# A transformer block on one core: the joining factors' two differences from one GpSimd subtraction with a reversed operand

## The chip, the cores and the metric

The kernel runs on one core of a Trainium2 chip. The metric is the device time of one execution in microseconds (us). The engines are named as the profile names them: PE (TensorE matmuls; PEld is its weight load), DVE (VectorE), ACT (ScalarE), POOL (GpSimd) and SP (SyncE, which here only issues DMAs). "SPq" is SP's queue of DMA issues. L517 is line 517 of the kernel before.

## The reference

All of it is fp32. x is (2, 1024, 256), the context (2, 154, 192), 16 heads of 64:

```python
h = _layernorm(x, ln1_g, ln1_b)
x = _attention(h, h, sa_wq, sa_wk, sa_wv, sa_wo, sa_bo) + x
h = _layernorm(x, ln2_g, ln2_b)
x = _attention(h, cond_emb, ca_wq, ca_wk, ca_wv, ca_wo, ca_bo) + x
h = _layernorm(x, ln3_g, ln3_b)
p = h @ ff_w1 + ff_b1
a, gate = (p[..., :D_FF], p[..., D_FF:])
h = a * jax.nn.gelu(gate, approximate=False) @ ff_w2 + ff_b2
return h + x
```

The attention is softmax(q k^T / 8) v over each head, followed by the output projection. The change lies in the softmax of the first attention, the self-attention, alone.

## The kernel before, in words

The program runs three stages one after the other: the self-attention (about 20 to 725 us of the profile), the cross-attention and the gated feed-forward. Each engine's instructions are written out by hand in a fixed order (`tc.manual_schedule()`, L1004), so that an instruction that waits holds up all that stands behind it on its engine.

**Self-attention.** A unit is one batch and one pair of heads; there are 16 units. Each unit takes 8 steps (L1062: `for p in range(SA)`, 128 steps in all), and a step handles two groups of 64 queries. In `scores` (L481, matmuls at L488) a group's score tile has 128 partitions: four blocks of 32 partitions, made of two sets of 32 queries by the two halves of the 1024 keys. A partition thus holds one query against one half of the keys (512), for both heads of the pair. The two halves of one query lie on two different blocks of partitions.

One step, `self_first(p)` (L642), goes as follows:

1. PE writes the scores of two groups into two PSUM tiles, L488. There are only two buffers, so that PE can write the next step's scores only when ACT has read these.
2. DVE takes the negated maximum over each half of the keys, L650, twice.
3. ACT takes the exponents with that maximum as bias and sums each row as it goes, L499, four times 128x512.
4. Four DMAs on SP's queue carry the maxima and sums to the partitions of the other half of the keys, `exchange`, L509.

The two halves of a query were scaled by different maxima. One step later they are joined (`scale_groups`, L590, which calls `join`, L513). `st` is a tile of [own or other half][maximum or sum][group, head], so 2 x 2 x 4 numbers on each partition. The join is a chain of tiny instructions:

- L517 and L518 on POOL: `dd` = the other half's negated maximum less the own one (first half of `dd`), and the reverse (second half), 128x4 each;
- L519 on POOL: the minimum of `dd` and 0, 128x8;
- L521 on ACT: `ee` = exp(dd), 128x8, which stands in ACT's order behind the four exponents of the current step;
- L523 on POOL: `zz` = ee times the sums, 128x8; L525 on POOL: `den` = the sum of both halves of `zz`, 128x4;
- L596 on DVE: `rd` = 1/den; then four times L600 on POOL: the exponents times `rd` and `ee`, 128x512.

DVE's order within a step is: two maxima (L650), two 32x32 block transposes of the weights scaled a step earlier (L614), sometimes the adding of an output projection (L469) or layer-norm statistics, and last the reciprocal L596. The maxima of the next step stand behind that reciprocal. PE's order within a step is: the scores, and then a piece of other work (the projections L357 and L388, the weighted values L535, the output projection L462).

What follows from the order is a loop over two steps: maxima, exponents, exchange by DMA, join, reciprocal, and behind the reciprocal the next maxima.

Of the kernel before, what the change touches and what calls it, by code (L numbers as in the profile page):

```python
# [10 lines left out]
ALU = mybir.AluOpType  # L11
# [7 lines left out]
def tile_transformer_block(ctx: ExitStack, tc: tile.TileContext, a: dict, out: bass.AP):  # L19
    nc = tc.nc  # L20
# [492 lines left out]
    def join(u, st):  # L513

        dd = small.tile([P, 2, 4], F32, tag="dd", name=f"dd_{u}")
        neg = st[:, :, 0].rearrange("p s i j -> p s (i j)")
        nc.gpsimd.tensor_tensor(dd[:, 0, :], neg[:, 1, :], neg[:, 0, :], ALU.subtract)  # L517
        nc.gpsimd.tensor_tensor(dd[:, 1, :], neg[:, 0, :], neg[:, 1, :], ALU.subtract)  # L518
        nc.gpsimd.tensor_scalar(dd, dd, 0.0, 1.0, op0=ALU.min, op1=ALU.mult)  # L519
        ee = small.tile([P, 2, 4], F32, tag="ee", name=f"ee_{u}")  # L520
        nc.scalar.activation(ee, dd, AF.Exp)  # L521
        zz = small.tile([P, 2, 4], F32, tag="zz", name=f"zz_{u}")
        nc.gpsimd.tensor_tensor(zz, ee, st[:, :, 1].rearrange("p s i j -> p s (i j)"), ALU.mult)  # L523
        den = small.tile([P, 4], F32, tag="den", name=f"den_{u}")
        nc.gpsimd.tensor_tensor(den, zz[:, 0, :], zz[:, 1, :], ALU.add)  # L525
        return ee, den
# [63 lines left out]
    def scale_groups(u, st, members):  # L590

        ee, den = join(u, st)

        def reciprocals():
            rd = small.tile([P, 4], F32, tag="rd", name=f"rd_{u}")
            nc.vector.reciprocal(rd, den)  # L596
            for i, pr in enumerate(members):
                for j in range(2):
                    c = 2 * i + j
                    nc.gpsimd.tensor_scalar(  # L600
                        pr[:, j, :], pr[:, j, :], rd[:, c:c + 1], ee[:, 0, c:c + 1],
                        op0=ALU.mult, op1=ALU.mult,
                    )
                groups.append(pr)

        return reciprocals
# [636 lines left out]
```

## Time and profile before

| what | value |
|---|---|
| time, median of 3 runs | 1113.07 us (1111.95 to 1114.58) |
| the profiled execution's own time | 1114.26 us |
| its span | 1112.5 us |
| self-attention, 20 to 720 us: busy PE / DVE / ACT / POOL | 690.3 / 634.2 / 463.3 / 526.8 of 700 us |
| instructions at L517, L518 | 128 each, 201 and 202 ns |
| granted TensorE clock, mean | 0.998 |

A busy time is the sum of an engine's instructions. A wait is the idle time of an engine before an instruction, put down to the one that released it. The chain of waits is followed back from the last instruction of the program: at each step to what released it, or to the instruction before it on its engine; what lies on it set the end of this execution, as far as the profile tells.

### The profile page before, as it was taken

How to read it: one execution, taken by the hardware profiler on the slowest of the kernel's cores; microseconds unless marked ns; L12 is line 12 of the kernel's file. 1: busy time of each engine (PE TensorE's matmuls, PEld its weight loads, DVE VectorE, ACT ScalarE, POOL GpSimd, SP SyncE). 2: the span in 40 equal slices, each digit the busy share in tenths (PEclk: the TensorE clock that was granted, in tenths of full speed). 3: DMA queues.
4: the chain of work that ended last, by engine and by line, in shares of the span. 5: the costliest groups of instructions: out<-in, count | busy, mean ns of one | idle time of the engine just before them, and what ended most of it. 6: DMA issues, size and time to landing. Idle time of an engine off the chain costs nothing.

```text
span 1112.5 us, 44903 instructions
## 1 busy us (share of the span) xinstructions
PE 1092.5 (98%) x18452; PEld 732.9 (66%) x18452; DVE 855.3 (77%) x1205; ACT 626.1 (56%) x2025; POOL 684.7 (62%) x1584
## 2 busy tenths in 40 slices
PE   8999999999999999999999999999999999999998
PEld 6555666556757555566565565566766677888887
DVE  4889999898988989999999989978777885422212
ACT  4666666766666656666666766565556553121111
POOL 2777777777878777777777877776656653220000
PEclk9999999999999999999999999999999999999999
DMA  2222212121112011111111111046765553000000
GB/s 81 69 56 58 56 28 52 41 53 42 34 42 49 14 41 37 33 42 33 32 42 24 41 33 26 21 98 159 166 153 136 117 116 79 10 11 10 20 10 19
DMA packets 103983, 60.73 MB, mean 55 GB/s; under 512 B 32218, under 2 KB 94562, under 8 KB 103778
## 3 DMA queue, kind: packets, MB, share of 16 engines
q1 hardware_dynamic: 102546, 57.20, 21.8%
q8 instruction: 146, 2.39, 0.9%
q10 hardware_dynamic: 1232, 0.66, 0.2%
q14 instruction: 59, 0.48, 0.1%
HBM read 27.91 MB, written 2.10 MB: 27 GB/s over the span
## 4 chain that ended last, share of the span: by engine, by line
PE 63%; ACT 9%; DMA 7%; POOL 7%; DVE 7%; issue 3%; SPq 3%; DVEq 0%; POOLq 0%; ACTq 0%
PE pa L959 10%; PE po L535 10%; PE s L488 10%; ACT p L499 8%; DMA st<-st 6%; PE pf L982 5%; PE py_ca L462 5%; DVE st L650 4%; PE pq_ca L357 4%; PE poc L877 4%; SPq L509 3%; PE py_sa L462 3%; PE sc L798 3%; PE pv_sa L388 3%; PE pk_sa L357 3%
## 5 line engine op out<-in xcount | busy, mean ns | idle before, releaser
L499 ACT ACTIVATE p<-s,st 128x512 f32<-128x512 f32 x512 | 345.3, 687 | 195.4 <-DVE st L650 185.2
L600 POOL TENSOR_SCALAR p<-p,rd,ee 128x512 f32<-128x512 f32 x512 | 387.7, 772 | 46.8 <-DVE rd L596 45.9
L650 DVE TENSOR_REDUCE st<-s 128x2 f32<-128x1024 f32 x256 | 300.9, 1216 | 22.6 <-PE s L488 9.7
L614 DVE STREAM_TRANSPOSE pT<-p 128x1024 f32<-128x1024 f32 x256 | 302.3, 1218 | 0.3 <-POOL p L600 0.3
L488 PE MATMUL s<-k_sa,q_sa 64*32 64x512 f32 x4096 | 263.9, 593 | 8.6 <-ACT p L499 7.6
L535 PE MATMUL po<-pT,v_sa 64*32 64x256 f32 x8192 | 241.2, 376 | 1.7 <-DVE pT L614 1.4
L535 PEld LDWEIGHTS po<-pT,v_sa 64*32 64x32 f32 x8192 | 178.1, 106 | 71.9 <-issue 19.2
L488 PEld LDWEIGHTS s<-k_sa,q_sa 64*32 64x32 f32 x4096 | 82.6, 106 | 113.5 <-ACT p L499 61.9
L814 ACT ACTIVATE p<-sc,neg 128x154 f32<-128x154 f32 x256 | 96.4, 406 | 83.5 <-DVE rden L822 78.4
L825 POOL TENSOR_SCALAR p<-p,rden 128x154 f32<-128x154 f32 x256 | 97.3, 401 | 71.6 <-DVE rden L822 71.3
L968 DVE SCALAR_TENSOR_TENSOR u<-pa,cols,gate 128x256 f32<-128x256 f32 x64 | 30.9, 483 | 123.1 <-ACT gate L965 123.1
L959 PE MATMUL pa<-hT_ln,wf 128*128 128x256 f32 x512 | 121.1, 380 | 0.0
L965 ACT ACTIVATE gate<-pa,cols 128x256 f32<-128x256 f32 x64 | 30.4, 475 | 147.4 <-PE pa L959 144.1
L959 PEld LDWEIGHTS pa<-hT_ln,wf 128*128 128x128 f32 x512 | 96.7, 190 | 13.8 <-issue 0.9
L499 ACT ACTIVATION_READ_ACCUMULATOR p<-s,st 128x1 f32 x512 | 103.9, 203 | 0.0
L388 PEld LDWEIGHTS pv_sa<-sa_wv,hT_ln 64*128 64x128 f32 x1024 | 59.0, 188 | 14.6 <-issue 5.0
L982 PE MATMUL pf<-wf,u 128*128 128x256 f32 x256 | 64.7, 379 | 0.0
L523 POOL TENSOR_TENSOR zz<-ee,st 128x8 f32<-128x8 f32 x128 | 26.0, 203 | 60.4 <-ACT ee L521 60.4
L388 PE MATMUL pv_sa<-sa_wv,hT_ln 64*128 64x128 f32 x1024 | 62.2, 275 | 0.3 <-ACT v_sa L397 0.3
L462 PE MATMUL py_sa<-sa_wo,o_sa 128*128 128x256 f32 x256 | 59.7, 385 | 0.0
L462 PE MATMUL py_ca<-ca_wo,o_ca 128*128 128x256 f32 x256 | 59.7, 381 | 0.0
L357 PE MATMUL pk_sa<-hT_ln,sa_wk 64*32 64x512 f32 x960 | 58.2, 591 | 1.0 <-DMA st<-st 0.8
(89 smaller groups left out, 1253.6 us busy)
## 6 DMA issues: line engine op xcount, KB each, us to landing
wf<-pT_ca SPq DMA_DIRECT2D x128, 128.0 KB, 2.4
st<-st SPq DMA_DIRECT2D x512, 1.0 KB, 1.8
v_sa<-v_sa SPq DMA_DIRECT2D x32, 256.0 KB, 3.8
sa_wq<-in_L_xattn_sa_wq_dram SPq DMA_DIRECT2D x32, 128.0 KB, 3.0
sa_wk<-in_L_xattn_sa_wk_dram SPq DMA_DIRECT2D x32, 128.0 KB, 2.9
sa_wv<-in_L_xattn_sa_wv_dram SPq DMA_DIRECT2D x32, 128.0 KB, 3.3
ca_wq<-in_L_xattn_ca_wq_dram SPq DMA_DIRECT2D x32, 128.0 KB, 3.8
wf<-in_L_xattn_ff_w_dram SPq DMA_DIRECT2D x12, 256.0 KB
```

Of the source, the lines that this page charges most:

```text
L357: nc.tensor.matmul(pq[r][f:f + m, at:at + n], lhsT=wt[own, c, f:f + m], rhs=h[own, c, t0:t0 + n], start=(c == 0), stop=(c == NH - 1), tile ...
L388: nc.tensor.matmul(pv[r][:, i * P:(i + 1) * P], lhsT=h[own, c, i * P:(i + 1) * P], rhs=wt[own, c, :], start=(c == 0), stop=(c == NH - 1), ...
L462: nc.tensor.matmul(py[:, e * D:(e + 1) * D], lhsT=o[:, i, (t + e) * P:(t + e + 1) * P], rhs=wo[kind][:, g * HP + i, :], start=(i == 0), st ...
L488: nc.tensor.matmul(sc[a4 * KB:(a4 + 1) * KB, j, :], lhsT=q[r, c:c + KB], rhs=k[r, h * HB:(h + 1) * HB], start=True, stop=True, tile_positi ...
L499: nc.scalar.activation(pr[:, j, :], sc[:, j, :], AF.Exp, bias=st[:, 0, 0, i, j:j + 1], accum_out=st[:, 0, 1, i, j:j + 1],)
L535: nc.tensor.matmul(po[a2][d:d + KB, :QH // 2], lhsT=v[r, t, e, d:d + KB], rhs=pT[r, d // DH * NK + n, :], start=(t == 0 and e == 0), stop= ...
L600: nc.gpsimd.tensor_scalar(pr[:, j, :], pr[:, j, :], rd[:, c:c + 1], ee[:, 0, c:c + 1], op0=ALU.mult, op1=ALU.mult,)
L614: nc.vector.transpose(halves[h][:, :, c:c + KB], groups.pop(0).rearrange("p j (n k) -> p (j n) k", k=KB))
L650: nc.vector.tensor_reduce(st[:, 0, 0, i, :], sc[i], AX.X, ALU.max, negate=True)
L825: nc.gpsimd.tensor_scalar(pr_[:, j, i, :T], pr_[:, j, i, :T], rden[:, j, i:i + 1], 1.0, op0=ALU.mult, op1=ALU.mult,)
L959: nc.tensor.matmul(pa[:, half, :TF * P], lhsT=w1[:, c, half * DF + f * P:half * DF + (f + 1) * P], rhs=h[:, c, t0 * P:(t0 + TF) * P], star ...
L982: nc.tensor.matmul(sums[blk][i][:, :D], lhsT=sums[blk, "u"][:, f, i * P:(i + 1) * P], rhs=w2[:, f, :], start=(f == 0), stop=(f == NF - 1),)
```

## The change

The two subtractions that write the two halves of `dd` become one that writes all of it. Its second operand is both halves in their order, its first the two halves in reverse order: on each partition 2 x 4 elements with steps of -8 and 1, from element 8 on, beside 2 x 4 elements with steps of 8 and 1 from element 0 on. The values are the same.

```diff
@@ -514,8 +514,7 @@
 
         dd = small.tile([P, 2, 4], F32, tag="dd", name=f"dd_{u}")
         neg = st[:, :, 0].rearrange("p s i j -> p s (i j)")
-        nc.gpsimd.tensor_tensor(dd[:, 0, :], neg[:, 1, :], neg[:, 0, :], ALU.subtract)
-        nc.gpsimd.tensor_tensor(dd[:, 1, :], neg[:, 0, :], neg[:, 1, :], ALU.subtract)
+        nc.gpsimd.tensor_tensor(dd, neg[:, ::-1, :], neg, ALU.subtract)
         nc.gpsimd.tensor_scalar(dd, dd, 0.0, 1.0, op0=ALU.min, op1=ALU.mult)
         ee = small.tile([P, 2, 4], F32, tag="ee", name=f"ee_{u}")
         nc.scalar.activation(ee, dd, AF.Exp)
```

In the built program POOL has 128 instructions fewer. The order on PE, DVE, ACT and SP is the same, and so are the semaphores that each instruction waits for; the new subtraction waits for what L517 waited for. All lines behind L517 move up by one.

## The prediction

> **What bounds the kernel now.** I read the busy times first, then the chain of waits, then the waits of each engine, and at last the chain's pieces near the changed lines.
>
> From the page, the busy times and the chain's shares by engine:
>
> ```profile
> PE 1092.5 (98%) x18452; PEld 732.9 (66%) x18452; DVE 855.3 (77%) x1205; ACT 626.1 (56%) x2025; POOL 684.7 (62%) x1584
> ...
> PE 63%; ACT 9%; DMA 7%; POOL 7%; DVE 7%; issue 3%; SPq 3%; DVEq 0%; POOLq 0%; ACTq 0%
> ```
>
> PE is busy for 98% of the span, so a naive reading gives a change on POOL nothing. But the chain lies on PE for only 63%; in the self-attention it often runs through maxima, exponents, exchange and join, and POOL holds 7% of the span on it. There two things run neck and neck: PE's stream (690.3 of the 700 us from 20 to 720) and the loop over two steps that the join belongs to (DVE 634.2 of 700).
>
> Who waits for the join, and who for its sequels (engine and line, released by; us in total, times, longest):
>
> ```profile
> DVE rd L596 <- POOL den L525: 39.6, 55, 3.5
> ...
> ACT ee L521 <- POOL dd L519: 29.7, 44, 1.8
> ```
>
> The exponent of `dd` waits for POOL in only 44 of 128 joins. In the others ACT is still at its four large exponents when `dd` is ready, and an earlier `dd` gains nothing there. DVE waits for `den` 55 times. Behind that reciprocal stand the next step's maxima, behind them the exponents, and for these PE waits:
>
> ```profile
> PE s L488 <- ACT p L499: 7.6, 18, 1.7
> ...
> PE po L535 <- DVE pT L614: 1.4, 1, 1.4
> ```
>
> These 9 us are most of what PE idles for in this stage, and so about the most that anything earlier in the loop can give back.
>
> **The change part by part.** It removes one POOL instruction from each of 128 joins, adds 4 elements to the other, and moves nothing: no DMA, no wait, no order on PE, DVE, ACT or SP. POOL's rows, and one join in the timeline (start us, us):
>
> ```profile
> L517 POOL TENSOR_TENSOR dd<-st x128: 193/201/209, 27.3 to 722.8; 128x4 f32<-128x4 f32 x128
> L518 POOL TENSOR_TENSOR dd<-st x128: 193/202/211, 27.5 to 723.0; 128x4 f32<-128x4 f32 x128
> ```
>
> ```profile
> 306.97 0.20 POOL L517 TENSOR_TENSOR dd<-st 128x4 f32<-128x4 f32 x1
> 307.12 0.20 POOL L518 TENSOR_TENSOR dd<-st 128x4 f32<-128x4 f32 x1
> ...
> 307.41 0.25 POOL L519 TENSOR_SCALAR dd<-dd 128x8 f32<-128x8 f32 x1
> ```
>
> What goes is not the duration of 0.20 but the distance between the starts: L518 starts 0.15 behind L517, since it depends on nothing of it and the two overlap; L519 needs both and starts 0.29 behind L518. Over all joins the median distances are 151 and 294 ns, together 445.
>
> After it, dd and the minimum are one dependent pair. The trace of before has no operand walked in reverse, so the price is bounded. From below: the contiguous L525 at 128x4, `den<-zz`, takes 201 ns, and starts 282 behind L523. Nearest: L523 is a two-input instruction on 128x8 whose second operand is also two pieces of four with a step of 8 between them:
>
> ```profile
> L523 POOL TENSOR_TENSOR zz<-ee,st 128x8 f32<-128x8 f32 x128 | 26.0, 203 | 60.4 <-ACT ee L521 60.4
> ...
> L245 POOL TENSOR_TENSOR rstd_ln<-var_ln,power 128x2 f32<-128x2 f32 x24 | 17.1, 712 | 6.7 <-DVE var_ln L241 5.0
> ```
>
> 203 against 201 ns: neither the four further elements nor the jump cost anything. From above: the slowest two-input instruction of so few elements, the power at L245, 712 ns. I take L523's price, so 294 ns to the minimum, and **0.151 us less per join**. Only the sign of the step is not shown by any row.
>
> [...]
>
> On the path: I went through the chain's pieces and counted where it passes L518. A pass looks like this (start us, us):
>
> ```profile
> 423.57 0.20 POOL dd L517
> 423.77 0.16 POOL dd L518
> 423.94 0.08 issue
> 424.02 0.26 POOL dd L519
> 424.30 0.22 ACT ee L521
> ```
>
> There are 30 passes of 128, 4.7 us in sum. At 0.151 (one pass is only 0.05 long) that is 29 x 0.151 + 0.05 = **4.4 us**, if PE has that much idle time to give back behind them. It has it only in places, so I cap each stretch by PE's waits at L488 and L535 in that stretch:
>
> | stretch, us | passes | x 0.151 | PE idle | taken |
> |---|---|---|---|---|
> | 20 to 70 | 3 and a part | 0.50 | 2.9 | 0.50 |
> | 72 | 1 | 0.15 | 0 | 0 |
> | 200 to 280 | 7 | 1.06 | 1.2 | 1.06 |
> | 400 to 435 | 5 | 0.76 | 1.0 | 0.76 |
> | 460 to 500 | 3 | 0.45 | 0.4 | 0.40 |
> | 540 to 600 | 6 | 0.91 | 0.5 | 0.50 |
> | 665 to 735 | 4 | 0.60 | 3.3 | 0.60 |
>
> Sum **3.8 us**. The other 98 joins are costed at nothing: ACT's exponents cover them. Without that cover, every join on the path, it would be 128 x 0.151 = 19 us, which PE's 9 us of idling rule out. What is late next, where a stall goes, is the exchange: four issues at L509 of some 0.6 us on SP's queue and 1.8 us to landing, which nothing here shortens.
>
> Against its own time, the profiled execution would go from 1114.26 (span 1112.5 and 1.8 around it) to 1110.4. It lies 1.2 above the median of the runs; the difference taken from the median, 1113.07 - 3.8, gives **1109.3 us**.
>
> **The rivals.**
>
> *PE takes over (0.24).* Where the loop gets shorter, PE's stream of matmuls is as long as before. For it: from 20 to 720 PE is busy 690.3 of 700, and most of its waits at L488 are short, 0.25 or so. Then only the end of the stage counts, where PE has to wait in any case: three joins in a row (695, 711.9 and 723.0) before the last weighted values. 3 x 0.151 = 0.45, so 1112.6. Against it: the passes cluster where PE does idle.
>
> *The reversed operand is dear (0.14).* This one makes it slower. Place: between the start of dd and that of the minimum; from 445 ns on, that is if the instruction is over 0.15 us dearer than L523, the change loses. At the upper bound, 712 + 92 (294 less 202) = 804 ns, each join is 0.36 later. 30 passes make 10.8 us, all 44 joins that ACT waits for 15.8, so 1124 to 1129. Against it is L523, whose pieces jump forward for free; for it, only that no row shows a negative step.
>
> *More than the sum (0.08).* At 698 us PE idles for 1.7 us, and from 701.3 to 704.8 the granted clock is 0.50, the only such dip of the stage. An idling of 1.6 us at 34 had no dip after it. If 0.15 less idling spares the dip, 3.4 us at half speed are up to 1.7 us more: with all 4.4 passes, 1107.0.
>
> That the change doesn't do what it says, I set aside: the built program has 128 POOL instructions fewer and the same waits.
>
> **How the numbers follow.** The forecast has 0.54. About 0.2% (2.2 us) is what a measurement of this kernel can tell from no change. Of the forecast's 0.54, 0.50 lie beyond that and 0.04 within; with the last rival, faster has 0.58. Within: 0.04 and 0.22 of "PE takes over", 0.26. Slower: 0.14, and 0.02 where shifted transfers cost PE more than the join gives: 0.16. The range leaves out the dear operand and a rest. Its low end is the median less 4.4, 1.7 and the runs' own scatter downward of 1.1: 1105.9. Its high end is 1112.6 and the scatter upward of 1.5: 1114.1.
>
> **What would show it.** The new row dd<-st at 128x8 near 203 ns and the minimum some 294 behind its start: the price is right; over 355 ns, it is the dear operand. ACT's wait for dd should fall by up to 44 x 0.15 = 6.6 from 29.7, DVE's wait for den by some 7 from 39.6, PE's wait at L488 from 7.6 to about 4. If the first two fall and the last does not, PE has taken over, or the exchange lands later. Wrong I am too if the loop's joins all come earlier and the exchange's issues meet other transfers on SP's queue.

## The result, and the profile after

| | before | after |
|---|---|---|
| median of 7 runs each, us | 1112.03 (1109.72 to 1114.58) | 1107.69 (1105.67 to 1108.84) |
| ratio, 95% interval | | 0.9959 (0.9948 to 0.9971) |
| profiled execution, own time / span | 1114.26 / 1112.5 | 1108.61 / 1106.7 |

The ratio is 4.6 us of 1112, with its interval 3.2 to 5.8. The forecast was 3.8 us less.

First the changed rows, the POOL instructions on `dd` of the kernel after (count, duration in ns min/median/max, first and last start), and one join of its timeline (start us, us):

```profile
L517 POOL TENSOR_TENSOR dd<-st x128: 193/200/211, 27.4 to 715.8; 128x8 f32<-128x8 f32 x128
L518 POOL TENSOR_SCALAR dd<-dd x128: 247/248/272, 27.7 to 716.1; 128x8 f32<-128x8 f32 x128
```

```profile
300.37 0.20 POOL L517 TENSOR_TENSOR dd<-st 128x8 f32<-128x8 f32 x1
300.66 0.25 POOL L518 TENSOR_SCALAR dd<-dd 128x8 f32<-128x8 f32 x1
300.94 0.21 ACT L520 ACTIVATE ee<-dd 128x8 f32<-128x8 f32 x1
301.23 0.20 POOL L522 TENSOR_TENSOR zz<-ee,st 128x8 f32<-128x8 f32 x1 [0.33 <-ACT ee L520]
```

The reversed operand takes 200 ns, and the minimum starts 292 ns behind it in the median, 285 to 303 over all joins. Before it was 445. In the joins where ACT waits for `dd`, the whole way from the start of `dd` to that of the reciprocal fell from 1534 to 1377 ns (medians worked out from the traces).

Then busy times and the chain of waits by engine, from the page of after:

```profile
PE 1088.1 (98%) x18452; PEld 721.6 (65%) x18452; DVE 854.5 (77%) x1205; ACT 624.6 (56%) x2025; POOL 662.2 (60%) x1456
...
PE 70%; ACT 8%; DMA 7%; DVE 5%; POOL 4%; SPq 3%; issue 3%; DVEq 0%; POOLq 0%; ACTq 0%
```

POOL went from 7% to 4% of the chain and DVE from 7 to 5; PE has 70% in place of 63. These shares are of one execution each, and kernel e1 below, as fast as after, has others, so they are no proof by themselves. PE's 18452 matmuls are the same ones, but its busy time fell from 1092.5 to 1088.1. Of the span's 5.8 us, 4.4 are "busy" PE time and 1.4 are PE idle time (20.0 before, 18.6 after).

And the waits of after (us, times, longest):

```profile
PEld s L488 <- ACT p L499: 51.6, 95, 2.5
...
DVE rd L595 <- POOL den L524: 29.6, 41, 3.2
...
ACT ee L520 <- POOL dd L518: 21.5, 36, 1.9
...
PE s L488 <- ACT p L499: 6.2, 13, 1.6
```

ACT's wait for `dd` fell by 8.2, DVE's for `den` by 10.0. PE's own wait at L488 fell by 1.4 only; the weight load's wait at the same matmuls fell by 10.3, from this row of before:

```profile
PEld s L488 <- ACT p L499: 61.9, 108, 2.5
```

### The profile page after: what moved, and what is told of

Read it like the earlier page. It is cut to its first block, busy times and chain, and to the rows that moved or that the text cites. A ratio compares the mean times of both kernels' runs of the same rounds, so it can differ in the third digit from the quotient of the medians.

```text
span 1106.7 us, 44775 instructions
## 1 busy us (share of the span) xinstructions
PE 1088.1 (98%) x18452; PEld 721.6 (65%) x18452; DVE 854.5 (77%) x1205; ACT 624.6 (56%) x2025; POOL 662.2 (60%) x1456
## 4 chain that ended last, share of the span: by engine, by line
PE 70%; ACT 8%; DMA 7%; DVE 5%; POOL 4%; SPq 3%; issue 3%; DVEq 0%; POOLq 0%; ACTq 0%
PE po L534 13%; PE s L488 12%; PE pa L958 10%; ACT p L499 7%; DMA st<-st 6%; PE pf L981 5%; PE py_ca L462 5%; PE pq_ca L357 4%; PE poc L876 4%; PE py_sa L462 4%; SPq L509 3%; DVE st L649 3%; PE pv_sa L388 3%; PE sc L797 3%; PE pk_sa L357 3%
## 5 line engine op out<-in xcount | busy, mean ns | idle before, releaser
L488 PE MATMUL s<-k_sa,q_sa 64*32 64x512 f32 x4096 | 258.7, 592 | 7.2 <-ACT p L499 6.2
L534 PEld LDWEIGHTS po<-pT,v_sa 64*32 64x32 f32 x8192 | 172.5, 107 | 78.7 <-issue 23.7
L488 PEld LDWEIGHTS s<-k_sa,q_sa 64*32 64x32 f32 x4096 | 80.6, 106 | 112.2 <-ACT p L499 51.6
L462 PEld LDWEIGHTS py_sa<-sa_wo,o_sa 128*128 128x128 f32 x256 | 47.3, 190 | 17.8 <-ACT v_sa L397 5.9
```

Source lines behind the costliest of these rows:

```text
L462: nc.tensor.matmul(py[:, e * D:(e + 1) * D], lhsT=o[:, i, (t + e) * P:(t + e + 1) * P], rhs=wo[kind][:, g * HP + i, :], start=(i == 0), st ...
L488: nc.tensor.matmul(sc[a4 * KB:(a4 + 1) * KB, j, :], lhsT=q[r, c:c + KB], rhs=k[r, h * HB:(h + 1) * HB], start=True, stop=True, tile_positi ...
L534: nc.tensor.matmul(po[a2][d:d + KB, :QH // 2], lhsT=v[r, t, e, d:d + KB], rhs=pT[r, d // DH * NK + n, :], start=(t == 0 and e == 0), stop= ...
```

## The experiments

The theory: the join lies on a loop over two steps that PE ends up waiting for, so the time follows the join's length. Rivals: POOL's load or count of instructions is what matters; the reversed operand has a hidden price; PE's stream is the bound and gives back only what it idles for. Ratios are to the kernel before, each timed beside it on the same chip. "Join" is the median from the start of `dd` to that of `rd` where ACT waits for `dd`, from the one profiled execution. The medians come from different chips and are not to be compared with one another; the ratios are.

| run | join, ns | ratio, 95% interval | median us |
|---|---|---|---|
| before | 1534 | 1 | |
| after | 1377 | 0.9959 (0.9948 to 0.9971) | 1107.7 |
| e1 spare behind den | 1377 | 0.9947 (0.9930 to 0.9965) | 1108.6 |
| e11 spare behind the minimum | 1377 | 0.9949 (0.9928 to 0.9969) | 1111.8 |
| e12 memset ahead of the minimum | 1390 | 0.9953 (0.9936 to 0.9969) | 1111.7 |
| e2 spare ahead of the minimum | 1410 | 0.9988 (0.9970 to 1.0006) | 1113.4 |
| e3 forward operands | 1376 | 0.9947 (0.9928 to 0.9966) | 1108.4 |
| e10 half of dd again | 1664 | 1.0061 (1.0038 to 1.0083) | 1124.1 |
| e5 three spares | 1708 | 1.0091 (1.0067 to 1.0114) | 1123.3 |
| e4 no cap (no minimum with 0) | 1025 | 0.9866 (0.9840 to 0.9892) | 1099.3 |

**POOL's load, or the join's length?**

```diff
e1_spare_off_chain, against after
         nc.gpsimd.tensor_tensor(den, zz[:, 0, :], zz[:, 1, :], ALU.add)
+        junk = small.tile([P, 4], F32, tag="junk", name=f"junk_{u}")
+        nc.gpsimd.tensor_tensor(junk, neg[:, 0, :], neg[:, 1, :], ALU.subtract)
```

> The changed kernel with one more POOL subtraction, 128x4 into a spare tile, right behind den (L524), where POOL idles some 0.3 us for the reciprocal in any case. POOL has as many instructions as before, but the chain from dd to rd is as short as after. If the join's length is what counts: as after, ratio 0.996 to the kernel before (0.994 to 0.998). If POOL's instruction count or its busy time counts, wherever the instruction stands: as before, 1.000.

As after, 0.9947. POOL is as busy as before the change (681.8 us against 684.7) and has its 1584 instructions again; neither costs anything behind `den`. Its join and its time are those of after, and yet PE has even less of the chain in its one profiled execution than before, so differences of some 10% in such shares say nothing by themselves:

```profile
PE 58%; ACT 11%; DVE 8%; DMA 7%; POOL 6%; SPq 4%; issue 4%; DVEq 0%; POOLq 0%; ACTq 0%
```

The same two lines behind the minimum, where POOL waits for ACT's exponent:

> The changed kernel with the spare subtraction behind the minimum, where POOL waits for ACT's exponent anyhow: the join is as long as after. If only the length from dd to rd counts: as after, 0.994 to 0.997. If any instruction more inside the join costs: 0.998 to 1.000, as with the spare instruction ahead of the minimum.

0.9949, again as after. So POOL's load is not the cause.

**Longer joins.** The same two lines between `dd` and the minimum, once (e2) and three times (e5):

> The changed kernel with the same spare subtraction between dd and the minimum, so that the reversed operand stays and the start of the minimum is about 0.15 us later again. If the join's length counts: as before, 0.999 to 1.001, with 440 to 450 ns from dd's start to the minimum's. If the gain came from something else that goes with the reversed instruction (fewer instructions is excluded here, since the count is that of before): still 0.996.

> The changed kernel with three spare 128x4 subtractions between dd and the minimum: about 0.45 us longer from dd to the minimum than after, 0.30 longer than before. If the loop's length counts in proportion to the passes on the chain: 30 x 0.30 = 9 us more than before, up to 44 x 0.30 = 13 since more joins come to bind: ratio 1.008 to 1.012. If PE's stream is the bound and the change gained only what PE idled: no more than the waits can take, 1.002 to 1.004.

e2 went back to 0.9988, but not in the way I expected. A join of its timeline:

```profile
301.52 0.20 POOL L517 TENSOR_TENSOR dd<-st 128x8 f32<-128x8 f32 x1
301.68 0.20 POOL L519 TENSOR_TENSOR junk<-st 128x4 f32<-128x4 f32 x1
301.84 0.25 POOL L520 TENSOR_SCALAR dd<-dd 128x8 f32<-128x8 f32 x1
```

The minimum starts 324 ns behind `dd`, not 445. It has to wait some 290 for the result of `dd` anyway, and a spare that it does not depend on fits into that. In the kernel before the second subtraction cost its 151 because the minimum depended on it. So e2's join is only 33 ns longer than after's, and by its length it should have kept about four fifths of the gain. e5 gave the ratio expected, 1.0091, but with less: its minimum starts 624 behind `dd`, so the join is 174 longer than before, not 300. Two further kernels put the question again:

```diff
e10_second_half_again, against after
         nc.gpsimd.tensor_tensor(dd, neg[:, ::-1, :], neg, ALU.subtract)
+        nc.gpsimd.tensor_tensor(dd[:, 1, :], neg[:, 0, :], neg[:, 1, :], ALU.subtract)

e12_memset_on_chain, against after, at the same place
+        junk = small.tile([P, 4], F32, tag="junk", name=f"junk_{u}")
+        nc.gpsimd.memset(junk, 0.0)
```

> The changed kernel with the second half of dd written a second time by a subtraction of 128x4, same values, which has to wait for the first: from dd to the minimum some 585 ns, 140 more than before and 293 more than after. If the time follows the join's length (about 30 us per us of it, by the change itself and by the kernel without the cap): 0.140 x 30 = 4.2 us more than before, 1.003 to 1.005. The spare instruction between dd and the minimum lengthened the join by only 33 ns against after and yet cost the whole gain; if an instruction more inside the join costs about 4 us beside its length, then here 1.007 or more.

> The changed kernel with a memset of a spare 128x4 tile between dd and the minimum, which reads nothing: some 20 to 40 ns more to the minimum. If the join's length counts: 1 us above after, 0.995 to 0.998. If it costs what the spare subtraction at this place cost: 0.998 to 1.000.

e10, whose spare has to wait for `dd` and on which the minimum depends, came to 1.0061: about 7 us for 130 ns, above the 1.003 to 1.005 expected, though its interval takes in 1.005. e12 kept the gain, 0.9953, so it is not any instruction at that place. Apart from e2, the time follows the join, but not on one line: after and e4 gain 29 us per us of join (4.6 for 0.157, 15 for 0.509), e10 and e5 lose 52 and 58. A longer join binds more often: the chain passes through 8 joins in e4, 22 in after, 31 before, 42 in e5 and 52 in e10 (counted from the chain's pieces, one profile each; of the last two e10's join is the shorter). Where e2's gain went stays open. Its interval just reaches what its length would give beside after (0.997), but beside e1 and e3, timed on the same chip and at 0.9947 each, its length would give some 0.996, and that lies outside. Its exchange made POOL wait 55.2 us against 44.9 in after, but in e4, which is fast, it is 56.1; and one profile does not tell chance from cause. So the large differences follow the join's length; that nothing else counts among the small ones is not shown.

**The reversed operand.**

```diff
e3_forward_operand, against after
-        nc.gpsimd.tensor_tensor(dd, neg[:, ::-1, :], neg, ALU.subtract)
+        nc.gpsimd.tensor_tensor(dd, neg, neg, ALU.subtract)
```

> The changed kernel with both operands in forward order: the differences are then all zero and the joining factors all one, so this part of the computation is left out in substance, while the instructions, shapes and waits are those of after. If walking in reverse costs nothing: dd's row at 200 ns, 292 ns to the minimum, and the time of after, 0.996. If it costs something that the row does not show (at the operand's read): faster than after by more than 0.2%, 0.993 or less.

From the groups of POOL in e3 (busy, mean ns, idle time before):

```profile
L517 POOL TENSOR_TENSOR dd<-st 128x8 f32<-128x8 f32 x128 | 25.5, 199 | 50.8 <-DMA st<-st 47.6 <-issue 2.4
```

199 against 200 ns, 291 against 292 to the minimum, 0.9947. Walking in reverse costs nothing that can be measured here.

**How far it goes: three times the saving.**

```diff
e4_no_cap, against after
-        dd = small.tile([P, 2, 4], F32, tag="dd", name=f"dd_{u}")
+        dd = small.tile([P, 4], F32, tag="dd", name=f"dd_{u}")
         neg = st[:, :, 0].rearrange("p s i j -> p s (i j)")
-        nc.gpsimd.tensor_tensor(dd, neg[:, ::-1, :], neg, ALU.subtract)
-        nc.gpsimd.tensor_scalar(dd, dd, 0.0, 1.0, op0=ALU.min, op1=ALU.mult)
+        sums = st[:, :, 1].rearrange("p s i j -> p s (i j)")
+        nc.gpsimd.tensor_tensor(dd, neg[:, 1, :], neg[:, 0, :], ALU.subtract)
...
+        nc.scalar.activation(ee[:, 0, :], dd, AF.Exp)
...
+        nc.gpsimd.tensor_tensor(zz, ee[:, 0, :], sums[:, 0, :], ALU.mult)
...
+        nc.gpsimd.tensor_tensor(den, zz, sums[:, 1, :], ALU.add)
```

> The join with the other half's maximum as the reference for both: one difference of 128x4, its exponent, times the own sum, plus the other sum. The minimum with 0 and the second factor go; the result is the same as long as two halves' maxima differ by less than what fp32's exp can hold. From dd's start to ee's some 0.30 us, against 0.60 after and 0.75 before: 0.45 less than before, three times the saving of the change. If the join is on the path in proportion: 3 x 4.4 = 13 us, ratio 0.988. If PE's stream takes over soon: little beyond after, 0.994 to 0.996. I expect something between, 0.991 to 0.993, since fewer joins bind the shorter they get.

0.9866, 15 us less (12.0 to 17.8): proportional and more than I expected. It is also the fastest kernel here that computes the block, under the condition named in its expectation. From its page, busy times and the chain by engine:

```profile
PE 1084.7 (99%) x18452; PEld 727.0 (66%) x18452; DVE 854.1 (78%) x1205; ACT 624.5 (57%) x2025; POOL 629.9 (57%) x1328
...
PE 88%; ACT 3%; DVE 3%; DMA 2%; POOL 1%; SPq 1%; issue 1%; DVEq 0%; POOLq 0%; ACTq 0%
```

The chain now lies on PE for 88%, and PE's busy time fell once more with the same matmuls. To see where PE's stream ends:

```diff
e6_no_cap_no_exchange, against e4_no_cap: no exchange, and the own half for the other
-        nc.gpsimd.tensor_tensor(dd, neg[:, 1, :], neg[:, 0, :], ALU.subtract)
+        nc.gpsimd.tensor_tensor(dd, neg[:, 0, :], neg[:, 0, :], ALU.subtract)
...
-        nc.gpsimd.tensor_tensor(den, zz, sums[:, 1, :], ALU.add)
+        nc.gpsimd.tensor_tensor(den, zz, sums[:, 0, :], ALU.add)
```

> The kernel without the cap, and without the exchange by DMA: the join takes each partition's own half for both, so the joining of the halves is left out in substance and the output is not the reference's. The loop over two steps has no DMA any more. This shows where PE's stream alone ends: if PE was the bound already without the cap, at most the 5 us that PE still idles there at L488 and L534 go, ratio 0.982 to 0.987; if stalls are still hidden inside PE's busy time, more goes, below 0.980. I expect 0.981.

0.9813 (0.9790 to 0.9836), 1092.1 us. The chain and the wait of the weight load:

```profile
PE 95%; DVE 2%; ACT 1%; POOL 1%; DMA 1%; issue 0%; DVEq 0%; SPq 0%; ACTq 0%
```

```profile
PEld s L488 <- ACT p L499: 10.6, 12, 2.3
```

With no exchange in the loop PE has the chain nearly alone. PE was busy for 98 or 99% of the span in every one of these kernels, but its stream as such needs some 20 us less than before.

**The exchange over two queues.**

```diff
e7_no_cap_two_queues, against e4_no_cap
-            nc.sync.dma_start(
+            (nc.sync if a4 < 2 else nc.scalar).dma_start(
```

> The kernel without the cap, with two of the four DMAs of each exchange issued from ACT's queue instead of SP's, so that two issues of 0.6 us stand behind one another in place of four and the last lands some 1.2 us earlier. If the exchange is what is next late: 2 to 5 us faster than without the cap alone, ratio 0.982 to 0.985. If the issues hold up ACT, whose next instructions are the copies that PE waits for: slower than without the cap alone, over 0.990.

0.9991 (0.9978 to 1.0003): all of e4's gain is lost. A step of its timeline:

```profile
301.85 0.21 ACT L520 ACTIVATE ee<-dd 128x4 f32<-128x4 f32 x1
302.00 1.17 ACTq L509 DMA_DIRECT2D st<-st  x2
...
303.21 0.65 ACT L634 COPY o_sa<-po 128x256 f32<-128x256 f32 x2 [1.15 <-PE s L488]
```

Two issues hold ACT for 1.17 us, and the copies that PE waits for stand behind them (the first copy starts where the issues end, at 303.2; the bracket names PE's scores, which that copy does not read). The exchange itself did come earlier: its last issue starts 0.68 us behind the last exponent, against 1.94 in e4 (medians worked out from the traces), and POOL's wait for it fell from 56.1 to 21.9 us. But PE's weight load at L357 waits 22.7 us for ACT's copies, against 2.5 in e4.

**Are the 30 passes places?** The single subtraction in only those 30 joins where the chain of before passed L518, and in only the other 98:

```diff
e8_only_the_30 (e9_only_the_98 has "not in"), against after
+        passes = (0, 3, 4, 6, 8, 32, 33, 34, 36, 42, 43, 44, 68, 69, 70, 71, 72, 79, 83, 84, 94, 95, 96, 97, 100, 102, 117, 122, 125, 127)
+        if u in passes:
             nc.gpsimd.tensor_tensor(dd, neg[:, ::-1, :], neg, ALU.subtract)
+        else:
+            nc.gpsimd.tensor_tensor(dd[:, 0, :], neg[:, 1, :], neg[:, 0, :], ALU.subtract)
+            nc.gpsimd.tensor_tensor(dd[:, 1, :], neg[:, 0, :], neg[:, 1, :], ALU.subtract)
```

> The reversed single subtraction only in the 30 joins at which the chain of the kernel before passed L518, the two subtractions in the other 98. If the passes are places fixed by the program's order: nearly all of the gain, 0.995 to 0.997. If it is the mean length of the join over the loop that counts, wherever: 30 of 128 of the gain, 0.999.

> The reverse: the single subtraction only in the 98 joins at which the chain did not pass. If the passes are fixed places: as before, 0.999 to 1.001. If the mean length counts: 98 of 128 of the gain, 0.996 to 0.997. If passes move to the neighbours as soon as those are the longer ones: between, 0.998.

0.9972 (0.9954 to 0.9990) with the 30, 0.9983 (0.9966 to 1.0001) with the 98: some 3.1 and 1.9 us, together about the whole. Per join that is 0.10 us against 0.02, which suggests that the chain points at the right places. It does not show it: the two intervals overlap, and both just take in what an even share per join would give (0.999 with the 30, 0.997 with the 98). Neither set carries the whole gain.

## Why the prediction was right, and which term was off

**The price per join** was right: 200 ns for 203, 292 to the minimum for 294, 0.153 saved for 0.151; e3 shows that the sign of the step costs nothing (199 ns forward, 200 in reverse). The rival "the reversed operand is dear" falls with that.

**The count of 30 passes** gave the right size; how far by luck is open. 29 x 0.151 + 0.05 = 4.4 us, uncapped, lies in the measured interval of 3.2 to 5.8, and so does the capped 3.8; e1, e3 and e11, with the same join to 1 ns, came to 5.7 to 5.9. For e4, whose join is 0.509 shorter than before, 30 x 0.509 = 15.3 against 15 measured, although only 8 joins are left on its chain: with a count that falls from 31 to 8 on the way the sum should be smaller, so this match is no proof of the count. As a list of places it is rougher still, as e8 and e9 show.

**The mis-sized term is the cap by PE's idle time.** I capped each stretch by PE's waits at L488 and L535 and took their 9 us as about the most that could come back. e4 got back 15 and e6 some 21. A busy PE hides stalls: in the profile of after a matmul at L488 lasts 592 ns in the mean, and PE counts as busy for as long, whether or not the next has started. Within a step the starts of the scores lie 7 ns apart in the median, but 482 of 3968 distances before and 435 after are over 100 ns and yet shorter than the matmul ahead, with no other matmul started between (worked out from the traces). The sums of the starts show what that comes to. From the first to the last of the 32 starts of a step's scores, summed over the 128 steps (worked out from the traces), it is 197.7 us in e5, 192.6 before, 187.3 after, 182.4 in e4 and 175.3 in e6, for the same 4096 matmuls. In the change itself that is 5.3 us less, where the spans differ by 5.8 and only 1.4 of them came out of PE's idle time. In the other kernels, too, this sum roughly follows the span of the profiled execution (186.7 us for 1106.9 in e1, 191.2 for 1109.0 in e12, 198.2 for 1119.0 in e10), but for e7 (196.7 for 1110.7).

The weight load's wait at L488 for ACT falls in the same order in the five kernels named first: 81.7, 61.9, 51.6, 29.1 and 10.6 us. It is no measure of the time by itself. In e12, which kept the gain, it is 62.6 us; and in e7, which is as slow as before, PE's weight load waits at L357 instead, and the row is short:

```profile
PEld s L488 <- ACT p L499: 17.3, 28, 1.5
```

**PE takes over** was the rival for 1112.6. It does take over, as far as the chain tells, but 20 us further down: at e6's 1092, with 95% of the chain on PE. **More than the sum** asked for the dip of the granted clock to go. In the profile of after that dip is gone (the same wait, now 1.55 us of idling up to 692.4, has none behind it), but one of the same length appears at 721.6 to 725.0, behind another wait; the two windows of after:

```profile
718.00:721.00 3.00, 1.81 (x16) 0.82 (x12) 2.02 (x4) 3.00 (x15) 3.00 (x6) 1.00 0.48 148
721.60:725.00 3.40, 3.20 (x64) 1.80 (x72) 2.96 (x6) 1.10 (x5) 3.40 (x11) 0.50 0.01 2
```

(the columns are window, its length, the busy times of PE, PEld, DVE, ACT and POOL, granted clock, DMA share and GB/s). Nothing was gained there. The granted clock on record for each timed execution says the same. Two executions of after had no such dip (1.000) and took 1107.4 us on average, three had one (0.998) and took 1107.1; of the kernel before, timed on three chips with at least four executions of either kind, those without were faster by 0.05 to 1.6 us. A dip more or less is not what gave 4.6.

**The signs.** ACT's and DVE's waits fell by 8.2 and 10.0, where I had 6.6 and 7; why by more is not shown. PE's wait at L488 was to fall from 7.6 to about 4 and fell to 6.2; in e1, e3 and e11, as fast as after, it is 8.5, 7.3 and 7.9. By the prediction's own sign, PE would have taken over or the exchange landed later, and yet the time fell: that sign rested on the same idle time as the cap.

## What to carry to other kernels

A tiny instruction on an engine that is busy for 62% can cost the kernel the distance that it adds between dependent starts, times its passes on the chain of waits (here 0.153 us and some 30 passes, for 4.6 us). Count the passes, and take the product as an estimate, since the count itself changes with the length. Don't cap it by PE's idle time, which fell by 1.4 us here where the span fell by 5.8; look at how far the starts of PE's matmuls lie apart (5.3 us less in sum). The weight load's waits show where PE is held up, but one row of one profile does not rank kernels (62.6 us at L488 in e12, 61.9 before). What a chain of small instructions costs is the distance between dependent starts, so merging two that the third depends on paid here (292 ns in place of 445), while a neighbour that nobody waits for may be free (0.9947 with a spare behind `den`). Before moving DMA issues to another engine's queue, ask which instruction there stands behind them: in e7 two issues held ACT for 1.17 us, and e4's gain was lost.

## What the runs showed of the hardware

On POOL, the join's fp32 TENSOR_TENSOR instructions took 198 to 203 ns each at 128x4 and at 128x8, the minimum (TENSOR_SCALAR, 128x8) 248, 254 in e12; in the kernel before an independent one started 151 ns behind the one ahead (L518 behind L517), dependent ones 282 (L525 behind L523) and 294 (L519 behind L518), all medians. The subtraction with an operand walked in reverse took 200 ns (after), with a forward one 199 (e3). A memset of a spare tile, between two dependent ones, delayed the second by 5 ns (297 in e12 against 292 in after). An issue of a 1 KB piece took ACT 0.53 us in the median of 256 in e7, and two in a row 1.17. A 1 KB piece of the exchange landed 1.7 to 3.8 us behind its issue in the kernel before, with a median of 1.8, where the profile tells the landing; 17 of the 28 transfers of such pieces on its chain of waits took over 2 us (3.61 us at 403, 3.44 at 708).
